# Attention scores as two float32r products of split queries and keys

## The chip, the cores and the metric

The kernel runs on one core of one Trainium2 chip. The metric is device time in microseconds (us) of one execution, the median of several. A core has TensorE (PE, matmul), VectorE (DVE), ScalarE (ACT), GpSimd (POOL) and SyncE (SP); here SP issues nearly all DMAs. Each engine works through a queue of its own, and semaphores order them against each other.

## The reference, cut to what matters

There are 16 sequences of 1024 nodes with 128 features, and for each a weighted adjacency of 1024 x 1024. Layer 0 is masked attention with 8 heads of 16 features; its result is weighted with the adjacency and normalised again. Layer 1 is three SAGE layers over an adjacency that a row-by-row "dilation" has thinned; it is left out below, since the change doesn't touch it.

```python
q = (x @ Wq.T + bq).reshape(bt, n, H, HD).transpose(0, 2, 1, 3)
k = (x @ Wk.T + bk).reshape(bt, n, H, HD).transpose(0, 2, 1, 3)
v = (x @ Wv.T + bv).reshape(bt, n, H, HD).transpose(0, 2, 1, 3)
scores = jnp.einsum('bhnd,bhmd->bhnm', q, k) / math.sqrt(HD)
mask = (adj == 0)[:, None, :, :]
scores = jnp.where(mask, -jnp.inf, scores)
attn = jax.nn.softmax(scores, axis=-1)
attn = attn * adj[:, None, :, :]
attn = attn / (attn.sum(axis=-1, keepdims=True) + 1e-08)
ctx = jnp.einsum('bhnm,bhmd->bhnd', attn, v)
...
return ctx @ Wo.T + bo
```

## The kernel before, in words

The kernel has an attention stage (about the first 2400 us), in which the dilation of the adjacency runs beside the attention, and a SAGE stage after it. In the attention stage the order of the work on TensorE, ScalarE and VectorE is the order in which the program writes it down; the order on SP's and GpSimd's queues is set by the scheduler of the build.

`attention()` loops over 256 steps: sequence `b` (16), half `c` of the query nodes (2, of 512 columns each), and block `m` of the key nodes (8, of 128 rows each). A step has two groups, `g` = 0 and 1, of four heads each. So there are 512 groups. The nodes of a key block lie on the 128 partitions and the query nodes along the free dimension. A group does the following.

- `scores(i, g)`: 16 products of 32 x 32 (L545) write the mask, a large negative number where the adjacency is zero, into PSUM, and four products (L551), one for each head, add the scores. The head with place `j` uses rows 32j to 32j+31 of the array.
- L589, on ScalarE: two exponentials `e` of 128 x 1024.
- L594, on VectorE: two products `w` of `e` with the transposed adjacency `aT`, 128 x 1024 each.
- `values` (L478 and L483): `w` times the values, and `e` times a column of 1e-8 (`eps8`), summed in PSUM over the blocks `m`. They are written one group late: after the scores of the next group.

A tile of 32 rows holds the features of two heads, 16 each, of which a group needs one. Before the change, `kT` has all 128 features as they come, and `qT` exists twice: once with the features of the even heads kept and the others multiplied by zero (`own`, with the bias `bq` likewise), and once the other way round (L307). So the 32 rows of a product have 16 that count.

`turn_over(i + 2)` prepares the adjacency of a step two steps ahead: four transposes (L496) into the PSUM bank `m`, a copy `aT` on ScalarE (L499), its store `aT_d` (L500), the 0/1 mask `nomask` (L503), and six copies on SP's queue (L507, L508) that turn the mask by 32, 64 and 96 partitions.

`prepare(b + 1)` makes `q`, `k` and `v` of the next sequence beside the steps of this one. It is a generator, and a step takes from it one piece of TensorE work (`True`), and after the exponentials and products of the group the matching copy out of PSUM (`"evict"`). Its pieces are `turned` (transposes of the normed input), `key`, `query` and `value`, each for both halves. `"half 1"` and `"half 0"` hold it back until the step loop is in that half, so that a buffer of `qT` is free. All these pieces use the one PSUM bank `m`.

`dilation()` runs in 8 blocks. A block has counting rounds (L817: one comparison `hit` on VectorE, then small matmuls `gone`), and then one item for each of the 16 sequences (L882: a scan `wr`, then `er`, transposes, and the stores and loads `mr_d`, `gl`, `gm`, `ad` on SP's queue). `beside_attention()` takes pieces of it into the queues of the engines between the groups, by a table of costs, so that both end together.

The tiles of short life lie in rings of buffers: a ring with the tag `mr` has 4 buffers and serves the temporaries of the dilation's blocks.

Of the kernel before, what the change touches and what calls it, by code (L numbers as in the profile page):

```python
# [9 lines left out]

F32 = mybir.dt.float32
BF = mybir.dt.bfloat16
F16 = mybir.dt.float16
U8 = mybir.dt.uint8
I32 = mybir.dt.int32
AF = mybir.ActivationFunctionType
ALU = mybir.AluOpType
AX = mybir.AxisListType
# [3 lines left out]
P = 128  # L22
# [12 lines left out]
def swept(ctx: ExitStack, tc: tile.TileContext, t: dict, out: bass.AP, flag: bass.AP):  # L35
# [11 lines left out]
    H = 8  # L47
# [118 lines left out]
    def first_part(p1):  # L166
# [30 lines left out]


        names = ("Wk", "Wv", "Wq", "Wo")
        raw = pool.tile([P, 4, D], F32, name="raw", tag="kT")  # L200
        for i, name in enumerate(names):
            nc.sync.dma_start(raw[:, i, :], t[f"L0_gnn_{name}"])
        attn_w = one.tile([P, 4, D], F32, name="attn_w")
        wts = {name: attn_w[:, i, :] for i, name in enumerate(names)}
        bk = one.tile([P, 1], F32, name="bk")
        nc.sync.dma_start(bk, t["L0_gnn_bk"].rearrange("(d o) -> d o", o=1))

        own = one.tile([P, 2], F32, name="own")
        nc.vector.tensor_reduce(
            own,  # L210
            ident.rearrange("p (j g d) -> p g j d", g=2, d=HD),
            AX.XY,
            ALU.add,
        )
        bq = one.tile([P, 3], F32, name="bq")
        nc.sync.dma_start(bq[:, 2:3], t["L0_gnn_bq"].rearrange("(d o) -> d o", o=1))
        nr_i = shared.tile([B * NB, P], I32, name="nr_i", tag="ad", bufs=2)
        nc.sync.dma_start(nr_i, nodemask.rearrange("b (k p) -> (b k) p", p=P))

        def turn_weights():  # L220
            wps = ps_d.tile([P, 4, D], F32, name="wps", tag="d")
            for i in range(4):
                nc.tensor.transpose(wps[:, i, :], raw[:, i, :], ident)
            yield
            nc.vector.tensor_copy(attn_w, wps)
            nc.vector.tensor_tensor(bq[:, 0:2], own, bq[:, 2:3].to_broadcast([P, 2]), ALU.mult)
            yield

        def node_masks():
# [8 lines left out]
            )  # L238


        v1_both = shared.tile([P, 2, NB, H, 32], F32, name="v1_both", tag="aT2")
        v1s = [v1_both[:, i] for i in range(2)]
        for v1 in v1s:
            nc.vector.memset(v1[:, :, :, HD:], 0.0)
            nc.vector.memset(v1[:, :, :, HD : HD + 1], 1.0)
        never = one.tile([P, P], BF, name="never")
        nc.vector.tensor_scalar(never, ident, -BIG, None, ALU.mult)

# [35 lines left out]
        def prepare(b):  # L284


            yield False
            xt = xts.pop(b)
            h = shared.tile([P, NB, D], F32, name=f"h_{b}", tag="s", bufs=2)
            hT = shared.tile([P, N], F32, name=f"hT_{b}", tag="s", bufs=2)  # L290

            def turned(c, bank=(ps_m, "m")):
                pt = bank[0].tile([P, 512], F32, name=f"pt_{b}_{c}", tag=bank[1])
                for i in range(HB):
                    nc.tensor.transpose(pt[:, i * P : (i + 1) * P], h[:, c * HB + i, :], ident)
                yield "evict"
                nc.scalar.copy(hT[:, c * HN : (c + 1) * HN], pt[:, :HN])


            kT = pool.tile([P, N], F32, name=f"kT_{b}", tag="kT")  # L300

            def query(c, bank=(ps_m, "m")):
                pq = bank[0].tile([P, 512], F32, name=f"pq_{b}_{c}", tag=bank[1])
                nc.tensor.matmul(pq, wts["Wq"], hT[:, c * HN : (c + 1) * HN], start=True, stop=True)
                yield "evict"
                for g in range(2):
                    nc.scalar.activation(  # L307
                        qTs[c][:, g, :], pq, AF.Identity, bias=bq[:, g : g + 1], scale=own[:, g : g + 1]
                    )

            def key(c, bank=(ps_m, "m")):
                cc = slice(c * HN, (c + 1) * HN)
                pk = bank[0].tile([P, 512], F32, name=f"pk_{b}_{c}", tag=bank[1])
                nc.tensor.matmul(pk, wts["Wk"], hT[:, cc], start=True, stop=True)
                yield "evict"
                nc.scalar.activation(kT[:, cc], pk, AF.Identity, bias=bk)

            v1 = v1s[b % 2]

            def value(c, bank=(ps_m, "m")):  # L320
                pv = bank[0].tile([P, HB, D], F32, name=f"pv_{b}_{c}", tag=bank[1])
                start_with(pv, bias3[:, 0, :])
                for i in range(HB):
                    n = (c * HB + i) * P
                    nc.tensor.matmul(
                        pv[:, i, :], hT[:, n : n + P], wts["Wv"], start=False, stop=(i == HB - 1)
                    )
                yield "evict"
                nc.scalar.copy(
                    v1[:, c * HB : (c + 1) * HB, :, :HD], pv.rearrange("p k (h d) -> p k h d", d=HD)  # L330
                )

            if b == 0:

                first = layer_norm_relu(h, xt, "a0", 0, HB)
                for _ in range(2):
                    next(first)
                yield "weights"
                yield from first
                yield "weights"  # L340
                yield "biases"
                yield from turned(0)
                yield "turn 1"
                second = layer_norm_relu(h, xt, "a0", HB, NB)
                for _ in range(2):
                    next(second)
                yield from key(0)
                qTs = [pool.tile([P, 2, HN], F32, name=f"qT_{b}_0", tag="qT")]
                yield from query(0, (ps_d, "d"))
                yield from second  # L350
                ready[b] = (xt, qTs, kT, v1)
                yield True
                yield from value(0, (ps_d, "d"))
                yield True
                yield from turned(1)
            else:
                yield from layer_norm_relu(h, xt, f"a{b}")
                for c in range(2):
                    yield True
                    yield from turned(c)  # L360
                for what in (key, value):
                    yield True
                    yield from what(0)

                yield "half 1"
                qTs = [pool.tile([P, 2, HN], F32, name=f"qT_{b}_0", tag="qT")]
                yield True
                yield from query(0)

            ready[b] = (xt, qTs, kT, v1)  # L370
            for what in (key, value):
                yield True
                yield from what(1)
            yield "half 0"
            qTs.append(pool.tile([P, 2, HN], F32, name=f"qT_{b}_1", tag="qT"))
            yield True
            yield from query(1)

        def conclude(b, c, acc, xt):

            yield False
            cx = small.tile([P, HB, H, HD], F32, name=f"cx_{b}_{c}", tag="cx", bufs=1)
            oTs = []
            for g in range(2):
                oT = small.tile([P, HN], F32, name=f"oT_{b}_{c}_{g}", tag="oT", bufs=2)
# [85 lines left out]
        def attention():  # L471
# [3 lines left out]
            def values(acc, v1, m, g, es, ws):  # L475

                for j in range(4):
                    nc.tensor.matmul(  # L478
                        acc[g][32 * j : 32 * j + 32, :], v1[:, m, 2 * j + g, :],
                        ws[j // 2][:, j % 2, :], start=(m == 0), stop=False,  # L480
                    )
                for j in range(4):
# [47 lines left out]
            def scores(i, g):  # L530
# [1 line left out]
                if made.get("of") == (i, g):  # L532
                    return made["scores"]
                b, c, m = turns[i]
                _, qTs, kT, _ = ready[b]
                nomask = tiles[i][1]
                mm = slice(m * P, (m + 1) * P)
                scs = [
                    ps_s.tile([P, 2, HN], F32, name=f"sc_{b}_{c}_{m}_{g}_{q}", tag="sc")
                    for q in range(2)  # L540
# [1 line left out]
                for j in range(4):  # L542
                    for r in range(4):
# [2 lines left out]
                            scs[j // 2][to : to + 32, j % 2, :], never[rows, rows], nomask[rows, j, :],  # L546
                            start=True, stop=False, tile_position=(32 * r, to),
                        )
                for j in range(4):
                    rows = slice(32 * j, 32 * j + 32)  # L550
                    nc.tensor.matmul(  # L551
                        scs[j // 2][:, j % 2, :], kT[rows, mm], qTs[c][rows, g, :],
                        start=False, stop=True, tile_position=(32 * j, 0),
                    )
                made["of"], made["scores"] = (i, g), scs
                return scs

# [73 lines left out]
        def dilation():  # L631
# [84 lines left out]
            for k in range(NB):  # L716
# [149 lines left out]
                more = k + 1 < NB  # L866
                if more:
                    open_block(k + 1)
                wrs, gms, ers, ets = {}, {}, {}, {}

                def known(b):

# [5 lines left out]
                for i in range(B + 2):  # L878
                    b = i
                    if b < B:  # L880
                        wrs[b] = pool.tile([P, N], F16, name=f"wr_{k}_{b}", tag="wr", bufs=2)
                        nc.vector.tensor_tensor_scan(  # L882
                            wrs[b], rk(b, 1, N + 1), rk(b, 2, N + 2), -1023.0, ALU.add, ALU.add
                        )
# [10 lines left out]
                        nc.scalar.activation(wrs[b], wrs[b], AF.Abs, bias=mid_at[:, b : b + 1])  # L895
                    b = i - 1
                    if 0 <= b < B:
                        er = ers[b] = pool.tile([P, N], BF, name=f"er_{k}_{b}", tag="er", bufs=3)
                        nc.vector.tensor_scalar(
                            er, wrs.pop(b), off[:, b : b + 1], allof[:, b : b + 1], ALU.is_equal, ALU.max  # L900
                        )
# [53 lines left out]
        def judge():  # L955
# [2 lines left out]
            still = small.tile([P, 3], F32, name="still", bufs=1)  # L958
            nc.vector.tensor_reduce(still[:, 0:1], changed, AX.X, ALU.add)
            rd = rden.rearrange("p a i h -> p (a i h)")  # L960
            fits = pool.tile([P, B * NB * H], F32, name="fits", tag="kT")
            nc.vector.tensor_scalar(fits, rd, 1e25, None, ALU.is_le)
            nc.vector.scalar_tensor_tensor(
                fits, rd, 1e-30, fits, ALU.is_ge, ALU.mult, accum_out=still[:, 1:2]
# [984 lines left out]
```

## Time and profile before

| | us |
|---|---|
| median of 3 runs (3537.39 to 3546.47) | 3541.1 |
| span of the profiled execution | 3538.5 |
| PE busy | 3433.7 (97%) |
| DVE busy | 3172.6 (90%) |
| ACT busy | 2289.3 (65%) |
| POOL busy | 177.6 (5%) |

The span goes from the first to the last instruction of the profiled execution. The execution's own time is not given apart from it; the span lies 2.6 us under the median of the runs. Busy shares are means over both stages. The end of a matmul is modelled in the profile, so a busy PE is not a PE at its peak: starts tell more than durations. "Idle before" in a group of instructions is the time in which its engine had nothing to do just before them, with the releaser that ended it. "SPq" are the instructions by which SP issues DMAs; they aren't counted as busy.

### The profile page before, as it was taken

What the parts mean: (1) busy time and instruction counts of PE and PEld (TensorE: products, weight loads), DVE (VectorE), ACT (ScalarE), POOL (GpSimd) and SP (SyncE); (2) the same over time, 40 slices, a digit from 0 to 9 for tenths busy, and PEclk for the clock granted to TensorE, in tenths of its full rate; (3) what the DMA queues carried; (4) which work ended last, traced back from release to release, by engine and by line L of the source; (5) the groups of instructions that cost most, each with busy time, mean ns of one, the idle gap of its engine ahead of it and who ended that gap; (6) DMA issues with size and microseconds to landing.
All of it is one profiled execution on the core that took longest, in us unless ns stands there. A gap on an engine that the chain in (4) does not pass through costs nothing. (4 is left out here: it accounts for less than half of the span.)

```text
span 3538.5 us, 86073 instructions
## 1 busy us (share of the span) xinstructions
PE 3433.7 (97%) x34855; PEld 1884.6 (53%) x34855; DVE 3172.6 (90%) x5254; ACT 2289.3 (65%) x3781; POOL 177.6 (5%) x253
## 2 busy tenths in 40 slices
PE   8999999999999999999999999999999899999997
PEld 2333333333333333333333333337999899989997
DVE  7999999999989999999999999997878788878886
ACT  7699689679769869968876885873222333322224
POOL 2000000000000000000000000000000000000000
PEclk9999999999999999999999999999999999999999
DMA  7356456447537636735753873677999799889996
GB/s 233 103 173 195 126 157 195 143 132 221 171 110 216 201 115 198 223 117 163 232 170 118 243 213 108 191 228 263 331 328 331 274 328 331 325 308 333 332 333 217
DMA packets 650121, 772.27 MB, mean 218 GB/s; under 512 B 173264, under 2 KB 569168, under 8 KB 637424
## 3 DMA queue, kind: packets, MB, share of 16 engines
q1 hardware_dynamic: 632672, 708.58, 62.1%
q0 software_dynamic: 15456, 57.30, 4.9%
q8 instruction: 275, 4.51, 0.5%
q14 instruction: 134, 1.10, 0.1%
q10 hardware_dynamic: 1584, 0.79, 0.1%
HBM read 508.50 MB, written 157.29 MB: 188 GB/s over the span
## 5 line engine op out<-in xcount | busy, mean ns | idle before, releaser
L594 DVE TENSOR_TENSOR w<-e,aT 128x1024 f32<-128x1024 f32 x1024 | 1203.7, 1217 | 98.0 <-ACT e L589 97.6
L589 ACT ACTIVATE e<-sc 128x1024 f32<-128x1024 f32 x1024 | 990.8, 1020 | 373.8 <-PE sc L551 369.5
L1106 PE MATMUL pg<-y,aT 128*128 128x128 f32 (+1 forms) x6144 | 737.3, 275 | 0.0
L1106 PEld LDWEIGHTS pg<-y,aT 128*128 128x128 f32 x6144 | 711.8, 192 | 0.0
L478 PE MATMUL acc<-w,v_both 128*32 128x512 f32 x4096 | 676.7, 606 | 10.9 <-DVE w L594 5.7
L483 PE MATMUL acc<-e,eps 128*32 128x512 f32 x4096 | 653.3, 594 | 0.0
L551 PE MATMUL sc<-qT,kT 32*128 32x512 f32 x4096 | 584.0, 640 | 0.3 <-ACT qT L307 0.3
L145 DVE SCALAR_TENSOR_TENSOR aT<-mr,aT 128x1024 f32<-128x1024 bf16 x384 | 458.7, 1216 | 0.0
L483 PEld LDWEIGHTS acc<-e,eps 128*32 128x32 f32 x4096 | 165.5, 110 | 295.0 <-issue 284.9
L1129 ACT ACTIVATE sq<-o 128x512 f32<-128x512 f32 x96 | 60.6, 631 | 361.6 <-DVE o L1124 361.6
L882 DVE TENSOR_TENSOR_SCAN wr<-rk 128x1024 f16<-128x1024 bf16 x128 | 291.6, 2278 | 0.0
L545 PEld LDWEIGHTS <-never 32*32 32x32 bf16 x8192 | 78.2, 87 | 340.1 <-issue 318.5
L545 PE MATMUL sc<-nomask,never 32*32 32x512 bf16 x8192 | 247.0, 385 | 10.8 <-ACT e L589 7.5
L478 PEld LDWEIGHTS acc<-w,v_both 128*32 128x32 f32 x4096 | 106.9, 108 | 241.0 <-DVE w L594 148.9
L551 PEld LDWEIGHTS sc<-qT,kT 32*128 32x128 f32 x4096 | 160.0, 183 | 116.9 <-issue 116.1
L496 PEld LDWEIGHTS pa<-ident,a 128*128 128x128 f32 x1024 | 107.8, 141 | 181.2 <-issue 136.5
L1147 ACT COPY hT<-pt 128x512 f32<-128x512 f32 x96 | 56.3, 586 | 224.2 <-PE pt L1143 214.3
L1124 DVE SCALAR_TENSOR_TENSOR o<-pg,rdeg,mine 128x128 f32<-128x128 f32 x384 | 108.1, 344 | 88.9 <-PE pg L1106 87.1
L895 ACT ACTIVATE wr<-wr,th 128x1024 f16<-128x1024 f16 x128 | 148.0, 1156 | 46.5 <-DVE wr L882 45.6
L496 PE MATMUL pa<-ident,a 128*128 128x128 f32 x1024 | 168.5, 287 | 6.5 <-DMA a<-in_adj 5.8
L503 ACT ACTIVATE nomask<-aT 128x512 bf16<-128x512 f32 x256 | 161.4, 630 | 8.1
L499 ACT COPY aT<-pa 128x512 f32<-128x512 f32 x256 | 151.5, 592 | 12.0 <-PE pa L496 6.2
(225 smaller groups left out, 3927.5 us busy)
## 6 DMA issues: line engine op xcount, KB each, us to landing
aT<-aT_d SPq DMA_DIRECT2D x94, 2048.0 KB, 8.9
mr<-mr_d SPq DMA_DIRECT2D x188, 512.0 KB, 5.8
aT_d<-aT SPq DMA_DIRECT2D x256, 256.0 KB, 4.2
a<-in_adj SPq DMA_DIRECT2D x253, 256.0 KB, 4.2
ad<-in_adj SPq DMA_DIRECT2D x112, 512.0 KB, 4.3
nomask<-nomask SPq DMA_DIRECT2D x512, 96.0 KB, 2.7
nomask<-nomask SPq DMA_DIRECT2D x512, 64.0 KB, 2.6
nomask<-nomask SPq DMA_DIRECT2D x512, 32.0 KB, 2.8
```

Of the source, the lines that this page charges most:

```text
L145: nc.vector.scalar_tensor_tensor(part, mrs[h][:, j : j + 2, :].rearrange("p j n -> p (j n)"), 0.0, part, ALU.is_equal, ALU.mult)
L478: nc.tensor.matmul(acc[g][32 * j : 32 * j + 32, :], v1[:, m, 2 * j + g, :], ws[j // 2][:, j % 2, :], start=(m == 0), stop=False,)
L483: nc.tensor.matmul(acc[g][32 * j : 32 * j + 32, :], eps8, es[j // 2][:, j % 2, :], start=False, stop=(m == NB - 1),)
L496: nc.tensor.transpose(pa[:, k * P : (k + 1) * P], a[:, k, :], ident)
L499: nc.scalar.copy(aT[:, 0, :], pa)
L503: nc.scalar.activation(nomask[:, 0, :], aT[:, 0, :], AF.Relu, bias=1.0, scale=-1e38, accum_out=zeros[:, i : i + 1])
L545: nc.tensor.matmul(scs[j // 2][to : to + 32, j % 2, :], never[rows, rows], nomask[rows, j, :], start=True, stop=False, tile_position=(32 * ...
L551: nc.tensor.matmul(scs[j // 2][:, j % 2, :], kT[rows, mm], qTs[c][rows, g, :], start=False, stop=True, tile_position=(32 * j, 0),)
L589: nc.scalar.activation(e, scs[q], AF.Exp, scale=1.0 / math.sqrt(HD))
L594: nc.vector.tensor_tensor(w, es[q], aT.to_broadcast([P, 2, HN]), ALU.mult)
L882: nc.vector.tensor_tensor_scan(wrs[b], rk(b, 1, N + 1), rk(b, 2, N + 2), -1023.0, ALU.add, ALU.add)
L1106: nc.tensor.matmul(pg[:, i // 2, at : at + width], aT[:, j, i * P : (i + 1) * P], y[:, j, :width], start=(j == 0), stop=(j == NB - 1),)
```

## The change

The scores are made from two halves of q and of k, high and low, that together give the float32 value. The high half is what ScalarE writes as float32r (`split_r[:, 0]`); the low half is the rest, that VectorE forms by adding the bias and subtracting the high half (`split_r[:, 1]`). Both lie in one buffer, `split_home`, of 128 x 2 x 512. From there 16 copies on SP's queue for each half `c` put the features in place: `key_back` puts the high half of a head's key on rows 32j to 32j+15 and the low half on rows 32j+16 to 32j+31, and `query_back` puts the same query on both. The columns of the weights `Wq` and `Wk` and their biases are sorted beforehand, even heads first, so that a head's 16 features are 16 partitions in a row. A head's scores are then two float32r products, with the high and the low half of the query, in place of one float32 product.

Room for the new tiles comes from three places. The values lie 17 columns a head instead of 32 (`HW`), so that a product's 32 columns reach into the next head's, into rows of the result that are not read; `cx` and `split_home` lie in what is left of that tile. `wr` and `er` of the dilation become the two halves of one buffer in the ring `mr`. The key tiles `kA` are a ring of three half-sequence tiles, the query tiles `qM` one of two. In `prepare`, a piece `key_back` or `query_back` follows one turn after its copy out of PSUM, and the order of `value` and `query` changes.

```diff
-        own = one.tile([P, 2], F32, name="own")
...
-        nc.sync.dma_start(bq[:, 2:3], t["L0_gnn_bq"].rearrange("(d o) -> d o", o=1))
+        bqk = one.tile([P, 2], F32, name="bqk")
+        for i, name in enumerate(("L0_gnn_bq", "L0_gnn_bk")):
+            by_g = t[name].rearrange("(j g d o) -> g j d o", g=2, d=HD, o=1)
+            for g in range(2):
+                for j in range(4):
+                    at = (4 * g + j) * HD
+                    nc.sync.dma_start(bqk[at : at + HD, i : i + 1], by_g[g, j])
...
-        v1_both = shared.tile([P, 2, NB, H, 32], F32, name="v1_both", tag="aT2")
...
+        HW = HD + 1
+        VW = H * HW + 16
+        both = shared.tile([P, 4096], F32, name="both", tag="aT2")
...
+        cx_home = both[:, free : free + HN]
+        split_home = both[:, free + HN : free + 3 * HN].rearrange("p (t n) -> p t n", t=2)
+        split_r = split_home.bitcast(F32R)
...
+            def halves(ps_tile, bias):
+                nc.scalar.activation(split_r[:, 0, :], ps_tile, AF.Identity, bias=bias)
+                nc.vector.scalar_tensor_tensor(
+                    split_r[:, 1, :], ps_tile, bias, split_home[:, 0, :], ALU.add, ALU.subtract
+                )
+
+            def by_head():
+                for g in range(2):
+                    for j in range(4):
+                        for i in range(2):
+                            here, there = (4 * g + j) * HD, 32 * j + HD * i
+                            yield g, i, split_home[here : here + HD], slice(there, there + HD)
...
                 yield "evict"
-                for g in range(2):
-                    nc.scalar.activation(
-                        qTs[c][:, g, :], pq, AF.Identity, bias=bq[:, g : g + 1], scale=own[:, g : g + 1]
-                    )
+                halves(pq, bq)
+
+            def query_back(c):
+                qs.append(pool.tile([P, 2, 2, HN], F32R, name=f"q_{b}_{c}", tag="qM"))
+                for g, _, piece, rows in by_head():
+                    nc.sync.dma_start(qs[c][rows, g].bitcast(F32), piece)
...
-                nc.scalar.activation(kT[:, cc], pk, AF.Identity, bias=bk)
+                halves(pk, bk)
+
+            def key_back(c):
+                ks.append(pool.tile([P, 2, HN], F32R, name=f"k_{b}_{c}", tag="kA", bufs=3))
+                for g, i, piece, rows in by_head():
+                    nc.sync.dma_start(ks[c][rows, g].bitcast(F32), piece[:, i])
...
-                for what in (key, value):
-                    yield True
-                    yield from what(0)
-
+                yield True
+                yield from key(0)
+                yield True
+                key_back(0)
+                yield from query(0)
                 yield "half 1"
...
+                query_back(0)
+                ready[b] = (xt, qs, ks, v1)
                 yield True
...
+                yield from value(0)
+
+            yield True
+            yield from key(1)
+            yield True
+            key_back(1)
+            yield from value(1)
             yield True
             yield from query(1)
+            yield "half 0"
+            query_back(1)
...
-                for j in range(4):
-                    rows = slice(32 * j, 32 * j + 32)
-                    nc.tensor.matmul(
-                        scs[j // 2][:, j % 2, :], kT[rows, mm], qTs[c][rows, g, :],
-                        start=False, stop=True, tile_position=(32 * j, 0),
-                    )
+                for half in range(2):
+                    for j in range(4):
+                        rows = slice(32 * j, 32 * j + 32)
+                        nc.tensor.matmul(
+                            scs[j // 2][:, j % 2, :], ks[m // HB][rows, g, mm], qs[c][rows, g, half, :],
+                            start=False, stop=(half == 1), tile_position=(32 * j, 0),
+                        )
...
-                        wrs[b] = pool.tile([P, N], F16, name=f"wr_{k}_{b}", tag="wr", bufs=2)
+                        pairs[b] = shared.tile([P, 2, N], BF, name=f"pair_{k}_{b}", tag="mr", bufs=4)
+                        wrs[b] = pairs[b][:, 0, :].bitcast(F16)
...
-                        er = ers[b] = pool.tile([P, N], BF, name=f"er_{k}_{b}", tag="er", bufs=3)
+                        er = ers[b] = pairs.pop(b)[:, 1, :]
```

## The prediction

> **What bounds the kernel now.** I read the groups by line first, then the busy time by stretch, then the waits of VectorE and ScalarE, then the timeline of TensorE and of SP's queue. The change lies in the attention stage, 0 to about 2400 us of the span; the stage after it holds none of the changed lines.
>
> ```profile
> L594 DVE TENSOR_TENSOR w<-e,aT 128x1024 f32<-128x1024 f32 x1024 | 1203.7, 1217 | 98.0 <-ACT e L589 97.6
> L589 ACT ACTIVATE e<-sc 128x1024 f32<-128x1024 f32 x1024 | 990.8, 1020 | 373.8 <-PE sc L551 369.5
> ...
> L551 PE MATMUL sc<-qT,kT 32*128 32x512 f32 x4096 | 584.0, 640 | 0.3 <-ACT qT L307 0.3
> ```
>
> The attention work is 512 groups (256 steps of four heads twice), so a step is about 9.3 us and a group 4.65. By stretch (PE, PEld, DVE, ACT, POOL busy, clock, DMA share, GB/s):
>
> ```profile
> 1300.00:1350.00 50.00, 49.52 (x526) 17.13 (x518) 42.85 (x36) 36.07 (x52) 0.00 (x0) 1.00 0.43 133
> 1050.00:1175.00 125.00, 122.98 (x1290) 44.83 (x1283) 123.91 (x183) 118.14 (x195) 6.06 (x6) 1.00 0.72 209
> ```
>
> TensorE looks full in both, but ends of matmuls are modelled, so its busy share can't decide. VectorE decides: in the second kind of stretch (the dilation's row items run beside attention) it is 99% busy and is the bound; in the first (the dilation's counting rounds) it is idle 7 of 50 us, so there the chain score product, exp, multiply is. How much idle time that makes in the stage, and what ends it, is in the waits (total, times, longest):
>
> ```profile
> DVE w L594 <- ACT e L589: 94.5, 81, 5.0
> ...
> ACT e L589 <- PE sc L551: 364.5, 280, 4.1
> ```
>
> So at most 94.5 us can be had from faster scores, however fast they become. One group on TensorE and SP's queue beside it:
>
> ```profile
> 1230.57 0.43 PE L545 MATMUL sc<-nomask,never 32*32 32x512 bf16 x16
> ...
> 1230.93 1.14 PE L551 MATMUL sc<-qT,kT 32*128 32x512 f32 x8
> ...
> 1232.00 0.66 PE L496 MATMUL pa<-ident,a 128*128 128x128 f32 x4
> ...
> 1235.30 0.53 SPq L507 DMA_DIRECT2D nomask<-nomask  x1
> ...
> 1235.88 0.59 SPq L508 DMA_DIRECT2D nomask<-nomask  x1
> ...
> 1236.52 0.59 SPq L507 DMA_DIRECT2D nomask<-nomask  x1
> ```
>
> From start to start the masks (16 products in one pass) take 0.36 us, the four score products 1.07. SP is busy 0.53 to 0.59 us for each copy inside SBUF, one every 0.64, whether it moves 32, 64 or 96 partitions.
>
> **What the Trainium skill says.** "FP8 and Floating Point Precision", TensorE Precision Notes: true FP32 takes four passes through the array. The trace agrees: two records for each of 2048 score products and 1.07 us where one pass took 0.36. "TensorE: Matmul & The Clock Gate", Architectural detail (engine queue depths): ScalarE and VectorE are strict FIFO. The trace of before shows no case where that costs much; the prediction rests on it. "DMA: Bandwidth & Descriptors", Anatomy of one DMA: a fixed cost of about 2 us, mostly the receipt, before the semaphore moves (stated for GpSimd's path). The trace, on SP's, has 2.6 to 2.8 us from issue to landing for the mask copies, which I use.
>
> **The change part by part.** 1. *Score products.* Two passes take the place of four. With 0.36 us for a pass with its switch of tiling, and (1.07 - 0.36) / 3 = 0.24 for each further one, the new group takes about 0.6, so 0.45 to 0.5 us go, in 512 groups. The end of the stage sees only VectorE's idle time: of 94.5 us, 5.0 are the start, and in 1300 to 1350 there are 7.15 us of idle in some 11.5 groups, 0.62 each, of which 0.47 would go (75%). I take **-70** us (0 to -95).
>
> 2. *VectorE.* One new instruction for each key and query half: 16 sequences x 2 x 2 = 64, 128x512 from PSUM. Nearest rows: L420 0.670 us; L1124 and L145 (128 columns 0.344, 1024 columns 1.216) give 0.72. 64 x 0.70 = **+45** (43 to 48), in full since VectorE has no slack left. ScalarE loses 32 x 2 x 0.789 (qT) and 32 x 0.693 (kT), gains 64 x 0.69: 28 us less, at nothing, since it has 35% free. It hides under L594.
>
> 3. *The new copies.* Each half of q or k goes through one buffer, split_home, and 16 copies on SP's queue: 64 x 16 = 1024, and 14 more for the biases. No row shows a copy of 16 partitions. Ends: 0.42 us from issue to issue, as for gl, gm, a (0.32 to 0.46 busy), and 0.64 as for nomask; below 0.42 nothing on this queue goes, so a gain is excluded. I take 0.53. SP's own sum is 1024 x 0.53 = 540 us on some 1440 (1536 nomask x 0.60, the rest near 0.43): 83% of the stage, not a bound by itself.
>
> 4. *The new wait.* In sequences 1 to 15, query(0) comes one step after key(0) and overwrites split_home, so both its instructions (ScalarE L312, VectorE L313 of the changed kernel) wait until all 16 copies of key(0) have landed. In the built program SP's order puts the next step's aT_d and six nomask copies between the two halves of those 16, and in even sequences about four DMAs of the dilation more. From VectorE's L313 of the key: 16 x 0.53 + 6 x 0.64 + 0.5 = 12.8 us of issuing (14.7 even); the last issue starts 0.5 earlier and lands 2.6 later: 14.9 (16.8); ScalarE's part 0.7: 15.6 (17.5). Meanwhile VectorE has only what stands ahead of L313 of the query: four L594 and two 1.22 us additions, 7.3 us (even: a scan of 2.28 and smaller pieces, 9.4). It then stands for 8.2 us, and behind it in its queue stand the next w and all dilation steps; behind ScalarE's the next exps, and TensorE waits for these and for the PSUM bank that L313 must free. 15 x 8.2 = **+123** (0.42: 15 x 6.4 = 96; 0.64: 15 x 9.9 = 148).
>
> 5. *What is late next.* The 16 query copies then stand ahead of the nomask copies of the next sequence's first step: 16 x 0.53 + 0.45 + 6 x 0.64 = 12.8, landing at 14.8 after L313. VectorE has 14 us of work before that step's w, and scores and exp need 2.4 of them: late by 3.1 in odd sequences, hidden in even ones (19 us of work). 15 x 1.6 = **+24** (0 to 45).
>
> 6. *The start.* Before, the first exp starts at 20.14 us. Now bias copies (14 x 0.42), then masks, then key copies (16 x 0.53 + 2), the query's two instructions, its 16 copies and landing follow one another and nothing covers them: first exp near 45: **+25** (21 to 29).
>
> 7. *At nothing:* the 17-column value tiles (same matmuls), cx in the same home, wr and er as pairs in the mr ring (a pair is reused four items on, stored two before; cover: two items, about 20 us), the kA and qM rings (their slots are free a half sequence earlier). If that cover goes, some us a block: -5 to +20 together.
>
> Sum: -70 + 45 + 123 + 24 + 25 = +147 on the span of 3538.5, which is 2.6 below the median 3541.1 of the three runs; I add the same 2.6 around it: 3688, rounded to **3685**.
>
> **The rivals.** *A, faster: TensorE is the true bound.* Its busy share is 97% and hardly any idle is recorded; if VectorE's 99% were time stretched by late products, all 512 x 0.5 = 256 us would count: -256 + 217 = -39, 3502. It decides from 0.42 us a group upwards (217 / 512). Against it: L594 is 1217 ns in every stretch, so VectorE's time isn't stretched, and its idle time is the ceiling. Chance 0.11.
> *B, mild: cheap copies.* Issue at 0.42 and all idle time gone: -95 + 43 + 96 + 0 + 21 = +65, 3606, and with the fixed mask copies partly out of the way down to 3550. For it: issue cost follows neither size nor partitions, and some rows are at 0.32. Chance 0.22.
> *C, worse: SP falls behind.* In even sequences 117 DMAs stand from the first key copy to the last query's 16, over five steps (49.5 us); at 0.53 and 0.55 they take 63; of the 14 us by which SP is late I guess 6 covered, and the late gl, gm and nomask stop VectorE for 8 us in seven sequences: +56, 3741. *D: the products are no faster* in this form: part 1 is gone, 3755. Together 0.12.
> No difference: gain and stalls cancel, 0.05.
>
> **How the numbers follow.** The forecast has 0.50 (own range 3630 to 3730). Its time is stated. The range takes in B and the edge of no change below, C and D above: 3540 to 3770, leaving out A and a little at both ends. A measurement of this kernel tells 0.3% (about 10 us) from no change: faster 0.11, same 0.05, slower 0.84.
>
> **What would show it.** Right: the score group at 0.55 to 0.65 us from start to start; L594's waits for e far under 94.5; VectorE's new line waiting for DMA or for ScalarE's half 100 us and more in total, in pieces of 6 to 10 us, 15 of them; 1024 copies at about 0.5 us on SP; first exp near 45 us. Wrong: that wait in pieces under 3 us (step 4), or a span of the attention stage under 2350 us, which only A gives.

## The result, and the profile after

The changed kernel takes 4002.7 us (median of 4 runs, 4001.8 to 4008.5), the kernel before 3540.9 in runs on the same chip: a ratio of 1.1305 (95% interval 1.129 to 1.1319). Slower was right; the forecast of 3685 was far too low, and its range ended at 3770. The profiled span is 4001.1 us.

All of the loss lies in the attention stage. The last `w` starts at 2411.5 us before and at 2872.1 us after: 460.6 us later, and the spans differ by 462.6. The groups of instructions of the changed kernel (busy time and mean of one, then the idle time of the engine before them and what ended it):

```profile
L629 DVE TENSOR_TENSOR w<-e,aT 128x1024 f32<-128x1024 f32 x1024 | 1204.3, 1217 | 231.6 <-ACT e L624 230.5
L624 ACT ACTIVATE e<-sc 128x1024 f32<-128x1024 f32 x1024 | 990.6, 1020 | 426.9 <-PE sc L586 425.6
...
L586 PE MATMUL sc<-q,k 32*128 32x512 f32 x4096 | 389.4, 453 | 17.2 <-DMA q<-both 17.2
...
L313 DVE SCALAR_TENSOR_TENSOR both<-pq,bqk,both 128x512 fp32r<-128x512 f32 x32 | 24.0, 750 | 228.1 <-ACT both L312 228.1
```

`w` and `e` take as long as before, so they don't run slower on VectorE or ScalarE; these engines wait more. The score products cost less (389.4 us of busy time where they had 584.0), yet VectorE waits 230.5 us for `e` where it waited 94.5, and as long again in its new line L313. The busy time of the stage says the same (us, then PE, PEld, DVE, ACT, POOL, the TensorE clock that was granted as a share of full speed, DMA share, GB/s):

```profile
0.00:2870.00 2870.00, 2318.66 (x25776) 888.70 (x25780) 2312.17 (x3476) 1901.22 (x2969) 132.60 (x167) 0.90 0.58 163
```

VectorE does 2312 us of work here against 2263 before, some 50 more, but in 460 us more time. TensorE's granted clock is 0.90 (1.00 before). What TensorE waits for in the stage (total, times, longest) shows who was late:

```profile
PE pa L530 <- DMA a<-in_adj: 195.4, 46, 11.3
PE pa L530 <- DVE both L313: 189.7, 33, 16.5
PE sc L579 <- DMA nomask<-nomask: 74.9, 74, 6.8
```

Two of the three are transfers that the change did not touch: the adjacency load `a` and the mask copies. Before, TensorE waited 5.8 us for `a` and 2.0 for the masks:

```profile
L496 PE MATMUL pa<-ident,a 128*128 128x128 f32 x1024 | 168.5, 287 | 6.5 <-DMA a<-in_adj 5.8
```

The third is the PSUM bank that L313 frees (x1 below still has 79 us of this wait).

`a` and the masks are both issued on SP. Once issued, they land no later than before (the last number is the median from issue to landing in us; the first two lines are before, the others after), so the transfers themselves are not slower:

```profile
a<-in_adj SPq DMA_DIRECT2D x253, 256.0 KB, 4.2
nomask<-nomask SPq DMA_DIRECT2D x512, 96.0 KB, 2.7
...
a<-in_adj SPq DMA_DIRECT2D x253, 256.0 KB, 3.7
nomask<-nomask SPq DMA_DIRECT2D x512, 96.0 KB, 2.5
```

In the chain that ended last, SP's issuing has 14% of the span and DMA another 10%:

```profile
PE 36%; DVE 27%; SPq 14%; DMA 10%; ACT 8%; issue 4%; ACTq 0%; DVEq 0%
```

So the question for the runs: is it the number of copies on SP's queue, or the wait of the engines for the one buffer `split_home`, as the forecast had it?

### The profile page after: what moved, and what is told of

The parts are those of the page before. It is cut to its first block, busy times and chain, and to the rows that moved or that the text cites. A ratio compares the mean times of both kernels' runs of the same rounds, so it can differ in the third digit from the quotient of the medians.

```text
span 4001.1 us, 87344 instructions
## 1 busy us (share of the span) xinstructions
PE 3393.9 (85%) x34855; PEld 1916.5 (48%) x34855; DVE 3222.9 (81%) x5318; ACT 2272.8 (57%) x3749; POOL 178.9 (4%) x253
## 4 chain that ended last, share of the span: by engine, by line
PE 36%; DVE 27%; SPq 14%; DMA 10%; ACT 8%; issue 4%; ACTq 0%; DVEq 0%
PE pg L1142 14%; DVE w L629 11%; SPq L345 5%; PE acc L512 4%; DMA nomask<-nomask 4%; ACT e L624 3%; PE acc L517 3%; SPq L542 3%; SPq L541 3%; DVE hit L852 3%; DVE pair L918 3%; PE sc L586 2%; PE pn L1113 2%; DMA a<-in_adj 2%; PE pa L530 2%
## 5 line engine op out<-in xcount | busy, mean ns | idle before, releaser
L629 DVE TENSOR_TENSOR w<-e,aT 128x1024 f32<-128x1024 f32 x1024 | 1204.3, 1217 | 231.6 <-ACT e L624 230.5
L512 PE MATMUL acc<-w,both 128*32 128x512 f32 x4096 | 700.0, 662 | 15.5 <-DVE w L629 10.8
L530 PE MATMUL pa<-ident,a 128*128 128x128 f32 x1024 | 192.4, 318 | 404.5 <-DMA a<-in_adj 195.4
L586 PE MATMUL sc<-q,k 32*128 32x512 f32 x4096 | 389.4, 453 | 17.2 <-DMA q<-both 17.2
L579 PE MATMUL sc<-nomask,never 32*32 32x512 bf16 x8192 | 302.6, 392 | 90.9 <-DMA nomask<-nomask 74.9
L530 PEld LDWEIGHTS pa<-ident,a 128*128 128x128 f32 x1024 | 124.0, 157 | 498.5 <-DVE both L313 206.3
L918 DVE TENSOR_TENSOR_SCAN pair<-rk 128x1024 f16<-128x1024 bf16 x128 | 291.5, 2278 | 0.0
L586 PEld LDWEIGHTS sc<-q,k 32*128 32x128 f32 x4096 | 160.6, 188 | 139.6 <-issue 120.4
L512 PEld LDWEIGHTS acc<-w,both 128*32 128x32 f32 x4096 | 102.1, 112 | 228.9 <-DVE w L629 128.3
L313 DVE SCALAR_TENSOR_TENSOR both<-pq,bqk,both 128x512 fp32r<-128x512 f32 x32 | 24.0, 750 | 228.1 <-ACT both L312 228.1
L312 ACT ACTIVATE both<-pq,bqk 128x512 fp32r<-128x512 f32 x32 | 22.0, 687 | 282.2 <-DMA k<-both 278.3
```

Source lines behind the costliest of these rows:

```text
L512: nc.tensor.matmul(acc[g][32 * j : 32 * j + 32, :], v1[:, m, (2 * j + g) * HW : (2 * j + g) * HW + 32], ws[j // 2][:, j % 2, :], start=(m ...
L530: nc.tensor.transpose(pa[:, k * P : (k + 1) * P], a[:, k, :], ident)
L579: nc.tensor.matmul(scs[j // 2][to : to + 32, j % 2, :], never[rows, rows], nomask[rows, j, :], start=True, stop=False, tile_position=(32 * ...
L586: nc.tensor.matmul(scs[j // 2][:, j % 2, :], ks[m // HB][rows, g, mm], qs[c][rows, g, half, :], start=False, stop=(half == 1), tile_positi ...
L629: nc.vector.tensor_tensor(w, es[q], aT.to_broadcast([P, 2, HN]), ALU.mult)
L918: nc.vector.tensor_tensor_scan(wrs[b], rk(b, 1, N + 1), rk(b, 2, N + 2), -1023.0, ALU.add, ALU.add)
```

## The experiments

Theory Q: SP's queue is the bound, and whatever is queued there comes late. Rival W, the forecast's own: the wait at `split_home` stops VectorE. A kernel with a second buffer beside `split_home`, which would take that wait away and leave the copies, was not run. So what W costs is known only from the runs below.

**Fewer copies (x1).** The changed kernel with whole-tile copies, 96 instead of 1024:

```diff
-                for g, _, piece, rows in by_head():
-                    nc.sync.dma_start(qs[c][rows, g].bitcast(F32), piece)
+                for g in range(2):
+                    nc.sync.dma_start(qs[c][:, g].bitcast(F32), split_home)
...
-                for g, i, piece, rows in by_head():
-                    nc.sync.dma_start(ks[c][rows, g].bitcast(F32), piece[:, i])
+                nc.sync.dma_start(ks[c].bitcast(F32), split_home)
```

> The changed kernel with whole-tile copies: one copy of 128 partitions for a key half and two for a query half, 96 in all, in place of 1024 copies of 16 partitions. The features are then not sorted by head, so the scores are those of other feature pairs; all waits, buffers and instructions else stay. Theory Q (the number of copies on SP's queue is the whole loss, by the wait for the one buffer and by what queues behind it): the loss goes, 3500 to 3560 us, VectorE's waits at L313 under 30 us in total, and the granted clock back to 0.98 or more. Rival L (the turn through a buffer and its landing costs by itself, however few copies): L313 keeps 100 us and more, 3650 or above. Rival P (float32r products or the added VectorE work are what is slow): near 4000.

Measured 3575.2 us, ratio 1.0097 (1.0077 to 1.0117), 15 us above the range of Q. The 928 copies fewer are worth 428 of the 462 us. VectorE's waits in the stage:

```profile
DVE w L628 <- ACT e L623: 65.2, 73, 7.3
...
DVE both L313 <- ACT both L312: 16.2, 4, 10.7
```

The buffer is still the only one, and still waited for, but for 16 us, 10.7 of them in one wait. This fits both theories, since a short burst also frees the buffer sooner.

**The copies without anyone waiting (x6).** x1 again, with 14 or 15 small copies that nobody reads behind each whole copy:

```diff
+        def more_copies(n, of):
+            for _ in range(n):
+                r, w = more[0] % 8 * HD, more[0] // 8 % 8 * HD
+                nc.sync.dma_start(spare[r : r + HD, w : w + HD], of[r : r + HD, :HD].bitcast(F32))
+                more[0] += 1
...
+                more_copies(14, qs[c][:, 0, 0])
...
+                more_copies(15, ks[c][:, 0])
```

> The whole-copy kernel again, and behind each whole copy 15 (key) or 14 (query) small copies of 16 partitions by 16 columns from the fresh tile into a spare corner that nobody reads: as many DMAs on SP's queue in the same bursts as in the changed kernel, but nobody waits for them. (Scores of other feature pairs here too.) If the wait for the one buffer (step 4) is what costs: about as the whole-copy kernel, within 40 us. If the load on SP's queue costs by itself (rival C, adjacency loads and masks late): 150 to 250 us above the whole-copy kernel, with TensorE waiting for a and nomask, and L313 waiting little.

Measured 4103.5 us, ratio 1.1595 (1.157 to 1.1621): as slow as the changed kernel and 100 us more, with 33 us of waiting at the buffer. It is 528 us above x1, where Q expected 150 to 250. W alone is out. The small copies here read what the whole copy has just written, so SP also stands until that has landed (91 us in all), and x6 overstates Q; x14 below is cleaner.

**Another queue (x4).** The changed kernel with all 1024 copies issued by GpSimd (`nc.gpsimd.dma_start` in `key_back` and `query_back`).

> The changed kernel with its 1024 copies on GpSimd's queue; SP's queue is as before the change, and the one buffer stays. If SP's load matters, TensorE's waits for a and nomask fall from 270 us to under 40. The wait at L313 stays or grows, since issuing on GpSimd is not known to be quicker: 230 us or more there, and 3700 to 3850 in all. If only the buffer wait mattered, the time would stay at 4000 or above.

Measured 3635.3 us (two runs), ratio 1.0265 (1.0234 to 1.0297), less than the 3700 to 3850 expected. The same copies through the same buffer cost 367 us less. TensorE waits 5.8 us for `a`, once, and 9.3 for the masks; VectorE's waits are

```profile
DVE w L629 <- ACT e L624: 83.4, 87, 8.1
DVE both L313 <- ACT both L312: 63.5, 15, 14.6
```

The wait of W is there, but small: of its 63.5 us, 18 are at the start of the kernel, and most of the rest is 11 pieces of 1.7 to 8.0 us at the first query of a sequence, where the forecast had 15 of 8.2. All in all this kernel is 60 us slower than x1.

**The products alone (x3).** The kernel before with `kT` and `qT` as float32r and two products a head, the second with a tile of zeros, so the scores are those of rounded q and k. None of the copies, waits and VectorE work of the change is in it.

```diff
-            kT = pool.tile([P, N], F32, name=f"kT_{b}", tag="kT")
+            kT = pool.tile([P, N], F32R, name=f"kT_{b}", tag="kT")
...
+                for half in range(2):
...
+                            scs[j // 2][:, j % 2, :], kT[rows, mm], low if half else qTs[c][rows, g, :],
```

> The kernel before, with kT and qT written as float32r and each head's score made by two float32r products, the second with a tile of zeros as its low half: it has the changed kernel's products, and none of its copies, waits or VectorE work. (The low half of q is left out, so the scores are rounded.) Step 1 says -70 us: 3470, between 3445 and 3541. Rival A (TensorE is the bound): 3285 to 3350. Rival D (products no faster): 3541.

Measured 3502.9 us, ratio 0.9895 (0.9874 to 0.9915): 38 us faster, not 70 (within the range of 3445 to 3541). On TensorE's timeline a group's score products take 0.67 us from the first start to the start of what follows, where they took 1.07:

```profile
1800.66 0.51 PE L556 MATMUL sc<-qT,kT 32*128 32x512 f32 x4
...
1800.99 0.40 PE L556 MATMUL sc<-none,kT 32*128 32x512 f32 x4
1801.33 0.42 PEld L499 LDWEIGHTS pa<-ident,a 128*128 128x128 f32 x4 [0.37 <-issue]
1801.33 0.66 PE L499 MATMUL pa<-ident,a 128*128 128x128 f32 x4
```

VectorE's wait for `e` only fell to

```profile
DVE w L599 <- ACT e L594: 65.6, 71, 5.2
```

**Half the copies (x9).** The changed kernel with pieces of 32 partitions, 8 copies for each half:

```diff
+                    for j in range(4):
+                        rows = slice(32 * j, 32 * j + 32)
+                        nc.sync.dma_start(qs[c][rows, g].bitcast(F32), split_home[rows])
```

> The changed kernel with pieces of 32 partitions instead of 16: 8 copies for each key and query half, 512 in all instead of 1024 (the heads are not sorted into their tiles, so the attention weights are not the reference's). It sets the dose between 96 copies (3575) and 1024 (4003). If every copy on SP costs the same wherever it stands (428 / 928 = 0.46 us each), 512 copies give 3575 + 416 x 0.46 = 3767. If SP's queue only matters once its work no longer fits between two steps (a queue near full), the loss is mostly in the last half: 3580 to 3680, VectorE's waits at L313 for the first query under 5 us each, and TensorE's waits for a and nomask nearly gone.

Measured 3715.1 us, ratio 1.0492 (1.0474 to 1.0509): between the two expectations. The first 416 copies cost 140 us (0.34 each), the next 512 cost 288 (0.56 each). This fits a price that rises towards the 0.63 us that a copy takes from issue to issue, as free time on SP runs out.

**The masks away (x10).** The changed kernel with only the six mask copies of a step on GpSimd's queue.

> The changed kernel with only the six mask copies of a step (1536 in all) issued by GpSimd; the 1024 key and query copies stay on SP. It tells whether the 1024 copies are slow for what they are (their buffer, their wait), or because they share SP with the masks. Theory of SP's sum: SP loses more work (1536 x 0.6 = 920 us) than the change gave it (600), so TensorE's waits for a (195 us) and nomask (75) go, and what is left is VectorE at L313, 16 copies in a row at 0.63 = 10 us and 2 of landing less 7 to 9 of cover, 15 x 4 = 60: 3575 + 60 = 3635 (3600 to 3680). Theory of the buffer alone: L313 keeps its 228 us of waits and the time stays over 3850.

Measured 3724.6 us, ratio 1.0524 (1.0506 to 1.0543): 278 us less than the changed kernel without touching one of its new copies, but 90 more than Q foretold. SP now has work for about 1360 us of 2592, so its sum cannot be what is left. TensorE's waits:

```profile
PE pa L530 <- DVE both L313: 121.7, 49, 8.9
PE pa L530 <- DMA a<-in_adj: 88.1, 19, 8.6
```

A burst of 16 copies still stands ahead of an `a`, and the buffer still holds up L313 (85 us). So besides the sum of SP's work, the place of a copy in the queue seems to count. The next runs part the two.

**Idle copies in the kernel before (x11, x12).** 1024 copies of 16 x 16 of a constant to a spare tile, written four behind the masks of each step (x11) or 16 behind each eviction of key and query (x12):

```diff
+                nc.sync.dma_start(spare[r : r + HD, w : w + HD], eps8[r : r + HD, :HD])
...
+                more_copies(4)
```

> The kernel before, with 4 idle copies (16 partitions by 16 columns of a constant to a spare tile that nobody reads) put on SP's queue behind the six mask copies of each of the 256 attention steps: 1024 in all, none in a burst, no buffer shared, nobody waiting for one. Before, SP is busy 1720 us of the 2412 of the attention stage, 1024 x 0.63 = 645 more make 2365. If only the sum counts and SP reaches 83% of the time (as the changed kernel and the one with half the copies do: 2382 of 2872, 2110 of 2587), the stage takes 2850 and the kernel 3980. If slack is used where it is (SP at 85 to 91% in the stretches of the dilation's row items, 55 to 70% elsewhere), only the full stretches pay: 3700 to 3800. If it is the bursts and the waits for them, and not SP's sum, 3541 to 3570.

> The kernel before, with the same 1024 idle copies in 64 bursts of 16, each at the place where a key or query half is evicted; still nobody waits for one and no buffer is shared. Sum alone at 83%: 3980, like the even ones. Sum and place: a burst of 10 us delays the a and the masks of the next steps, and in the full stretches nothing is caught up: 3850 to 4000, above the even ones, TensorE's waits for a and nomask 150 to 300 us in total. If the wait for the one buffer (VectorE at L313) makes the loss of the changed kernel: under 3650.

Measured 4036.8 us, ratio 1.1401 (1.1382 to 1.142), and 4047.4, ratio 1.1434 (1.1415 to 1.1453). Both are above every range expected, and they did not do what they were made for. Nothing ties such a copy to its place, so the scheduler put all of them early; the tile view of x11 (durations, first and last start):

```profile
L265 SPq DMA_DIRECT2D spare<-eps x1024: 507/587/2222, 12.9 to 1148.1; - x171
```

What they show: copies that nobody waits for, in no shared buffer, cost about 500 us merely by standing ahead of others on SP.

**Idle copies tied to their place (x13, x14).** The same, but each reads what was just made there, 4 a step from `aT` (x13), or 16 behind each key and query half from `kT` or `qT` (x14):

```diff
+                more_copies(4, aT[:, 0, :])
```
```diff
+                more_copies(16, qTs[c][:, 1, :])
...
+                more_copies(16, kT[:, cc])
```

> The idle copies on constants were all issued in the first 1150 us of the stage, since nothing tied them to their place. Here each idle copy reads 16x16 of the step's own aT, so that 4 stand behind the masks in every one of the 256 steps (1024 in all, none in a burst, nobody waits for one, no shared buffer; the rest is the kernel before). SP's busy time before: 1720 of 2412 us, 85 to 91% in the stretches with row items, 52 to 70% in the others. If the sum decides at the 83% that the changed kernel reaches: 3980. If slack is used where it is: each step gains 2.5 us of SP work, full stretches pay in full, the others nothing or little: 3650 to 3800. If bursts and waits for them are what costs: under 3570.

> The same 1024 idle copies in 64 bursts of 16 behind the eviction of each key and query half, tied to their place by reading it (kernel before otherwise; nobody waits for a copy, no shared buffer). Sum alone: 3980, the same as the even ones. Place too: above the even ones by 100 us or more, 3850 to 4000, with TensorE's waits for a and nomask of 200 us and more. If the changed kernel's loss is its wait for split_home: under 3650.

Measured 3839.2 us, ratio 1.0843 (1.0825 to 1.0861), and 3979.9, ratio 1.1238 (1.1219 to 1.1257). The first is 39 us above the range for slack that is used where it is; the second lies where sum and place together were expected, and that the two differ excludes the sum alone. So 1024 copies on SP in the kernel before cost 298 us spread out and 439 in 64 bursts: 298 for the sum, 141 more for the place. The bursts of x14 are whole, those of the changed kernel in part broken up by mask copies. In x14, VectorE's and TensorE's largest waits in the stage are

```profile
DVE w L604 <- ACT e L599: 384.1, 153, 9.6
```
```profile
PE sc L555 <- DMA nomask<-nomask: 221.4, 108, 10.3
```

No engine in x14 waits for a copy, and the 439 us are nearly what the 928 copies cost in the changed kernel (428).

**The low half on GpSimd (x7, x8).** x1 (x7) and x4 (x8) with GpSimd making the low half:

```diff
+                nc.scalar.activation(split_home[:, 1, :], ps_tile, AF.Identity, bias=bias)
...
-                nc.vector.scalar_tensor_tensor(
-                    split_r[:, 1, :], ps_tile, bias, split_home[:, 0, :], ALU.add, ALU.subtract
-                )
+                nc.gpsimd.tensor_tensor(split_home[:, 1, :], split_home[:, 1, :], split_home[:, 0, :], ALU.subtract)
```

> The kernel with whole-tile copies (3575) with the low half of keys and queries made by GpSimd instead of VectorE: ScalarE writes the biased value and its rounding, GpSimd subtracts them. VectorE loses 64 x 0.75 = 48 us of work and never waits in that line. If VectorE is the stage's bound (step 2 of the prediction: 64 instructions in full), the time falls by 35 to 60 us to 3515 to 3540, under the kernel before or equal to it. If TensorE or ScalarE set the end there, it stays at 3575 within 10.

> All of the changed kernel's work, with the 1024 copies on GpSimd's queue (3635 so) and the low half made by GpSimd too. VectorE loses 48 us of work and the 63 us that it waits at L313; ScalarE still waits there for the buffer, now also through GpSimd's slower subtraction. Expected 3560 (3530 to 3600) if VectorE's standing at L313 is what the buffer costs; 3620 to 3660 if ScalarE's and TensorE's waits for the same buffer cost as much without it.

Measured 3578.0 us, ratio 1.0104 (1.0087 to 1.0121), no gain over x1; and 3674.1, ratio 1.0376 (1.0358 to 1.0393), slower than x4 and above both ranges. The first is the number expected if TensorE or ScalarE set the end, but the trace shows another reason. VectorE lost 48 us of work, but its busy time in x7's stage is 2316 us against 2306 in x1: other instructions became longer. In x7 one `w` takes up to 2312 ns, where the longest was 1227:

```profile
L627 DVE TENSOR_TENSOR w<-e,aT x1024: 1191/1219/2312, 36.9 to 2446.9; 128x1024 f32<-128x1024 f32 x171
...
L768 DVE TENSOR_TENSOR_SCAN w<-go_on,up x16: 2258/2284/3370, 83.1 to 2140.5; 128x1024 f16<-128x1024 bf16 x16
```

The Trainium skill, "SBUF — State Buffer", section "SBUF: two separate sides", says that GpSimd and a VectorE operation with two SBUF inputs exclude each other for a whole instruction. The trace agrees: against the medians of x1, 54 of VectorE's instructions in x7 are longer by 0.3 us or more, 53 of them overlap one of the 64 subtractions on GpSimd, and together they are longer by 52 us, where 48 were saved. So x7 says nothing against step 2 of the prediction; it moved the cost and got it back as longer instructions.

## Why the prediction was wrong

**Step 3 failed:** "83% of the stage, not a bound by itself". Two things were wrong in it.

The price: the copies took the dear end. SP's row in the changed kernel has 0.587 us as the median of one, and the median from start to start within a burst is 0.63, not 0.53 (16 in a row, below, take 10.55 us from the start of the first to the end of the last, which is 0.66 from start to start). The rest of SP's work was undersized as well: adding up SP's issues of before, with the pauses of under 0.2 us between two of them, gives about 1700 us in the stage, not 1440 (the expectations above have 1720). With 1024 x 0.63 = 645 that is 2345 of 2412 us, or 97%. In the changed kernel the same sum is 2407 of 2872 us (84%), in x9 2089 of 2581 (81%), in x14 2402 of 2855 (84%); with the copies spread evenly (x13) it is 2457 of 2710 (91%). The rest of the time SP stands for what it is to send. In the changed kernel its longest waits are for a free buffer of `a` and for `aT`:

```profile
SPq L188 <- PE pa L530: 105.3, 45, 6.8
SPq L534 <- ACT aT L533: 96.9, 64, 5.5
```

So SP waits for TensorE and ScalarE, these wait for SP, and SP's share stays under 100%. A share of 81 to 91% was a bound here, as taking work off SP (x1, x4, x10) and putting work on it (x13, x14) shows.

The mean: 1700 of 2412 is 70%, but by windows of 100 us SP has 81 to 91% in nearly a third of the stage before (7 of 24), where the dilation's row items run, and 53 to 75% in the rest. SP's timeline of before in such a step (start, duration):

```profile
1365.23 0.33 SPq L690 DMA_DIRECT2D gl<-mr_d  x1
1365.66 0.38 SPq L663 DMA_DIRECT2D ad<-in_adj  x1
...
1367.09 0.38 SPq L187 DMA_DIRECT2D a<-in_adj  x1
...
1368.29 0.53 SPq L507 DMA_DIRECT2D nomask<-nomask  x1
...
1373.90 0.39 SPq L912 DMA_DIRECT2D mr_d<-er  x1
1374.93 0.32 SPq L690 DMA_DIRECT2D gl<-mr_d  x1
```

From one `gl` to the next is 9.7 us, one attention step, and SP pauses once, for 0.6 us. A burst of 10 us put in here finds next to no free time in which to catch up. The changed kernel a little earlier in its own course:

```profile
1277.27 8.71 SPq L345 DMA_DIRECT2D k<-both  x12
...
1298.76 10.55 SPq L333 DMA_DIRECT2D q<-both  x16
1309.41 0.53 SPq L534 DMA_DIRECT2D aT_d<-aT  x1
1310.05 0.53 SPq L541 DMA_DIRECT2D nomask<-nomask  x1
...
1317.18 0.43 SPq L188 DMA_DIRECT2D a<-in_adj  x1
```

and TensorE waiting for just these (the idle time is in the brackets):

```profile
1312.59 0.55 PE L579 MATMUL sc<-nomask,never 32*32 32x512 bf16 x4 [2.12 <-DMA nomask<-nomask]
...
1321.72 1.08 PE L530 MATMUL pa<-ident,a 128*128 128x128 f32 x4 [4.59 <-DMA a<-in_adj]
```

The Trainium skill, "Perfetto Trace Analysis", section "What 'DMA-bound' means", names this as one kind of DMA-bound kernel: the issuing engine's sequencer track (its row of issuing instructions) is solid DMA slices, which are generation of descriptors and not movement of data. The trace agrees in part: the DMA engines are busy 58% of the stage before and after, at 163 GB/s after, while SP's row is filled to 84%, and to as much as 98% in a window of 100 us. So it was the bound without being solid. Another page, "DMA: Bandwidth & Descriptors", section "Issuing engines are not separate DMA queues", says that issuing from several engines saves only issue time, "usually small relative to the DMA itself". For one copy that holds, 0.59 us of issuing against 2.0 to 2.4 from issue to landing. But issues on one queue add up, and this queue had little room: issuing the 1024 copies from GpSimd saved 367 us (x4), and the measurement decides.

**Rival C** had the mechanism, "SP falls behind", at 3741. It had SP 14 us late in an even sequence, guessed 6 of them covered, and let 8 count in 7 sequences. It took 0.53 for a copy, looked at the first halves of key and query only, and left the odd sequences out. The runs have 428 us for the 928 copies: 0.46 us each, and 0.56 each for the last 512 (x9), close to the 0.63 that one takes from issue to issue. Little of it is covered.

**The sum, term by term.** x3, x1 and the changed kernel give it in three pieces, each the difference of two measured times:

| | predicted | measured |
|---|---|---|
| products (step 1) | -70 | -38 (x3) |
| split, order, start, without the many copies | +45 and part of +25 | +72 (x1 less x3) |
| 928 of the 1024 copies (steps 3 to 5, rest of 6) | +123, +24 and the rest of +25 | +428 (changed less x1) |

That "slower" came true was in good part luck: the main term of the forecast, the wait in step 4, was to make +123 of the +147, and with SP relieved, copies and wait together cost 60 (x4 less x1).

- **Step 1** was right in kind and mis-sized. A group fell from 1.07 to 0.67 us, not 0.6. Of 94.5 us of waits for `e`, 29 went. What ends the other 65.6 was not tried. In the changed kernel even this gain can't be seen, since TensorE waits for `a` and the masks.
- **Step 2** holds: 64 instructions of 0.743 to 0.751 us, 48 us, and VectorE's work in the stage rose by 51. That the end sees it in full was not measured apart, but x1 fits: -38 + 48 + 18 (its first `w` starts at 38.8 us instead of 21.2) + 16 (waits at L313) = 44, and x1 is at +34.
- **Step 4** saw the wait and its place, and the size roughly. VectorE waited 230.4 us at L313:

```profile
DVE w L629 <- ACT e L624: 230.5, 133, 8.7
DVE both L313 <- ACT both L312: 230.4, 33, 19.1
```

  The first query of sequences 1 to 15 has 149 us of it: 11 to 15 us in even sequences, 3 to 9 in odd ones (forecast 15 of 8.2). The second query, which the step left out, has about 60, and the start 21. But the step took this wait for the price. It is only where part of the lateness shows: in x14 there is no such wait, and VectorE waits 384 us for `e` instead.
- **Step 5** can't be told apart from the rest.
- **Step 6** holds: the first exp starts at 45.7 us, 25.6 later than before.
- **Step 7**: nothing in x1 or x4 asks for more than zero.
- **Rival A** is out: with faster products alone the gain was 38 us and not 256, nor the 205 that 512 x 0.40 would make. **B** is out by the issue price (its floor of 0.42 was not quite one either: `gl` to `gm` goes in 0.37 before), **D** by the 0.67 us.

Of the signs that it named for being right, the first exp came as forecast. But the waits of `w` for `e`, which were to lie far under 94.5 us, rose to 230.5, and there the missing cost showed. The list of what would make the forecast wrong named too short a wait at L313 and a stage that is too short. It had no line for SP, though step 3 had SP at 83% already.

No exact version here beats the kernel before. In this form the low halves cost VectorE 48 us and the products give back 38, so even free copies would leave about +10, an estimate from these two numbers; the best measured of those that keep the split exact is x4 with 3635. x3 is faster than before, but scores from rounded values.

## What to carry to other kernels

Add up the issue time of a queue as carefully as the busy time of an engine, from start to start, and by stretch and not over the stage: a queue at 70% on average had stretches at 90%, and 1024 copies of 0.63 us, unread and unwaited for, cost 298 to 439 us there. When a change puts many small DMAs on a queue, ask what else stands in it, and try the idle queue first. And a new wait in the trace is not yet its cause: put the suspected load in without the wait, as x14 did, before believing it.

## What the runs showed of the hardware

- SP takes 0.59 us (median) to issue a copy inside SBUF of 16 x 16 elements (x13) as of 16 partitions by 1024 (the query copies); a mask copy of 96 partitions by 512 bfloat16 takes 0.53 or 0.59, by its place among the six. GpSimd issued the same query and key copies in 0.48 us each (x4), and they landed in 3.3 to 4.1 us instead of 2.0 to 2.4.
- TensorE's granted clock was lower in the kernels in which it stalled more: 1.00 in the stage before, 0.99 in x1, 0.93 in x14, 0.90 in the changed kernel. The four transposes after a long stall take 1.08 us (1321.72 above) instead of 0.66. How much of the loss this makes was not measured apart.
- GpSimd's subtraction of two 128x512 tiles lasts 1.25 to 5.0 us as recorded in x7, and the 54 of VectorE's instructions that it lengthened grew by 1.07 us in the median.
